# Holding one result in weight tiles, three heads in one 12 KB tile, and zeroing one shared scratch tensor once

## The chip, the cores and the metric

The kernel runs on one core of one Trainium2 chip. The metric is the device time of one execution in microseconds, the median of several runs. A profile of one further execution shows every instruction with its start and duration.

## The reference

Input is x of shape (4, 384, 32, 32): four images ("batches"), 384 channels, 1024 tokens each. Two layers follow one another, each with a residual around a mixing part and around a feed-forward part.

```python
# layer 0
x = x + L0_conv(ln_c(x))      # four-direction selective scan, 16 states, then layernorm and GELU
t = tokens(x)
t = t + L0_ffn(ln_t(t))       # 4 experts, top 2 per token: y = gelu(t w1 + b1) w2 + b2, weighted by the gate
# layer 1
x = x + L1_conv(ln_c(x))      # attention with 8 heads of 64; queries, keys and values share one projection
t = t + L1_ffn(ln_t(t))       # W = kron(c_fc_1, c_fc_2); gelu(t W^T) times kron(c_proj_1, c_proj_2)^T
```

The scan of layer 0 is `h = h * exp(dt * A) + dt * u * B`, `y = h . C`, over 1024 positions in each of four directions. All arithmetic is float32.

## The kernel before

The four batches go through two parts. The **scan** (`scan_layer`, `chunk`) takes a batch in 8 units (4 directions by 2 halves of the tokens); a unit has 3 channel chunks of 4 steps, so a batch has 96 steps. In a step POOL multiplies the scanned input with B (L440) and part of the states with C (L468), ACT makes the decay (L449), DVE runs the recurrence (L454) and the other products with C (L461), and PE adds the states up into `acc` (L475). Its inputs come back from DRAM in `dtr` (L424) and `bcs` (L350), issued by SP.

The **tail** (`tail_batch`) of a batch is everything else:

- `route`: `first` zeroes the scratch tensor `rows` (`clear`, L599, 19 DMAs of 192 KB) and turns the batch into token order; `second` chooses the experts, and POOL scatters each normalized token into its two rows of `rows` by indirect DMA (L685).
- `experts`: 11 slots, 8 of 256 rows and 3 of 128. A slot gathers its rows (`xs`, L925), loads an expert's weights as four `w1` tiles (L900) and four `w2` tiles (L908) of 576 KB each, computes `hs` (L954, L962, L967 or L959) and `y` (L975, L979), and writes `made` (L982).
- `combine` and `prologue`: POOL gathers the two results of each token (L1005), PE adds them with their gates (L1012), and the layernorm's result is transposed into `xc`.
- `attention`: four pairs of heads; each has a projection (weights L1069, matmuls L1076), scores (L1099), exponentials (L1105), the sum over values (L1145) and a division, into one `att` tile.
- `last_layers`: the output projection (L1198) with its residual gives `x2` (L1204); then the second feed-forward, in two halves of the tokens and two groups of hidden rows each (`hs`, L1259, L1265, L1268; L1276; L1284), whose result is added to `x2` (L1286) and stored (`out`, L1287). Its weights are `wa`, `wb` and `wc` (L1169 to L1173). For batches 0 and 1 the next batch's `route` steps stand inside it.

The tail of batch b runs beside the scan of batch b + 1. The tail of batch 3 comes last and uses a larger set of buffers (`WIDE`).

Tiles of the tail come from pools by tag, each with a number of buffers. A tile takes a buffer that is free, and its first writer waits until the last reader of what was there is done.

```python
NARROW = {"kw": 8, "k12": 2, "k4": 5, "got": 1, "bb": 2}
WIDE = {"kw": 10, "k12": 3, "k4": 4, "got": 2, "bb": 2}
...
att = room.tile([P, L], "kw", "att")
x2 = room.tile([P, DC, L], "k12", "x2")
hs = room.tile([P, FC, size], "k12", "hs")
```

"kw" tiles hold 4.5 KB a partition: the experts' weights, `wa`, `wb`, `wc`, projections, `got` and `att`. "k12" tiles hold 12 KB: `hs`, the combined tokens, `xc`, squares and `x2`.

The order of each engine's instructions is fixed at build time by a planner that simulates the program's progress. Parts marked with `high_priority` come earlier in it. On the chip each engine, and SP's queue of DMA issues, goes through its list strictly in order. The second branch of `build`, `second_layer_exact`, runs only if a softmax sum overflows; it doesn't run here, and the constant `EXACT` belongs to it.

Of the kernel before, what the change touches and what calls it, by code (L numbers as in the profile page):

```python
# [9 lines left out]
F32 = mybir.dt.float32  # L10
# [7 lines left out]
P = 128  # L18
# [62 lines left out]

NARROW = {"kw": 8, "k12": 2, "k4": 5, "got": 1, "bb": 2}
WIDE = {"kw": 10, "k12": 3, "k4": 4, "got": 2, "bb": 2}
EXACT = {"kw": 4, "k12": 2, "k4": 4, "got": 2}

FORWARD = 20000

# [28 lines left out]
class Body:  # L116
# [430 lines left out]
    def moe_consts(self, room):  # L547
        nc, a, wp = self.nc, self.a, self.const


        turn = wp.tile([P, DC, P + NE], F32, tag="turn", name="turn")
        wg = turn[:, :, P:]
        nc.sync.dma_start(out=wg, in_=a["wg"].rearrange("(c p) e -> p c e", p=P))
        for c in range(DC):
            nc.vector.tensor_copy(turn[:, c, :P], self.ident)
        ps = room.bank("p", "wg_ps")
        for c in range(DC):
            nc.tensor.matmul(ps[:, :NE], self.ones, wg[:, c, :], start=(c == 0), stop=(c == DC - 1))
        for c in range(DC):
            nc.vector.scalar_tensor_tensor(  # L560
                wg[:, c, :], ps[:, :NE], -1.0 / D, wg[:, c, :], op0=ALU.mult, op1=ALU.add
            )
        self.turn = turn
        bg = wp.tile([P, NE], F32, tag="bg", name="bg")
        nc.sync.dma_start(out=bg, in_=a["bg"].partition_broadcast(P))
        self.bg = bg

        def count(name, shape, pattern, base=0, channel=0):
            i = wp.tile([P, *shape], I32, tag=name, name=name + "_i")
            nc.gpsimd.iota(i, pattern=pattern, base=base, channel_multiplier=channel)  # L570
            f = i.bitcast(F32)
            nc.vector.tensor_copy(f, i)
            return f


        before = count("before", [P], [[1, P]], channel=-1)
        nc.vector.tensor_scalar(before, before, 0.0, None, op0=ALU.is_gt)
        self.before = before
        lower = count("lower", [NE, NE], [[1, NE], [-1, NE]])
        nc.vector.tensor_scalar(lower, lower, 0.0, None, op0=ALU.is_gt)  # L580
        self.lower = lower
        self.full = count("full", [L // P], [[P, L // P]])
        self.slot_at = count("slot_at", [NSLOT], [[1, NSLOT]])


        size = NROW
        self.zero = wp.tile([P, P], F32, tag="zero", name="zero")
        nc.gpsimd.memset(self.zero, 0.0)
        self.rows, self.made = [], []
        for b in range(B):  # L590
            self.rows.append(self.dram.tile([size, D], F32, tag=f"rows{b}", name=f"rows{b}"))
            self.made.append(self.dram.tile([size, D], F32, tag=f"made{b}", name=f"made{b}"))

    def clear(self, b):

        nc = self.nc
        self.zeroed = []
        for at in range(0, NROW, P):
            ins = nc.sync.dma_start(  # L599
                out=self.rows[b][at : at + P, :].rearrange("p (c d) -> p c d", c=DC),  # L600
                in_=self.zero.unsqueeze(1).to_broadcast([P, DC, P]),
            ).ins
            self.depend(ins, self.under_way[b])
            self.zeroed.append(ins)
# [8 lines left out]
    def route(self, b, x1, room):  # L613

        def forward():
            return nullcontext() if 0 < b < B - 1 else self.tc.high_priority(offset=FORWARD)

        parts = self.spread(b, x1, room)

        def first():  # L620
            self.clear(b)
            with forward():
                next(parts)

        def second():
            with forward():
                self.place, self.slots = next(parts)

        return first, second

    def spread(self, b, x1, room):
# [44 lines left out]
        for m in range(MB):  # L676
            if m % 2 == 0:
                xt = room.tile([P, 2, D], "k4", "xt")
                nc.sync.dma_start(out=xt, in_=self.tokens(b)[:, m : m + 2, :])
            nc.scalar.activation(  # L680
                xt[:, m % 2, :], xt[:, m % 2, :], AF.Identity,
                bias=less[:, m : m + 1], scale=rstd[:, m : m + 1],
            )
            for k in range(TOP):
                put = nc.gpsimd.indirect_dma_start(  # L685
                    out=self.rows[b][:, :],
                    out_offset=bass.IndirectOffsetOnAxis(ap=pos[:, k, m : m + 1], axis=0),
                    in_=xt[:, m % 2, :], in_offset=None,
                ).ins
                for other in placed:  # L690
                    self.tc.declare_no_dep(put, other, reason="rows of different tokens")
                for other in self.zeroed:
                    self.depend(put, other)
                placed.append(put)
        yield (pos, gate), (expert, placed)

    def places(self, sc, room):
# [184 lines left out]
    def experts(self, b, routed, room):  # L882

        nc, a = self.nc, self.a
        rows, made = self.rows[b], self.made[b]
        expert, placed = routed
        nw = 4
        wf = FC // nw
# [32 lines left out]
        def gather(s):  # L921
            at, size = extent(s)
            xs = room.tile([P, size // P, D], "k4", "xs")
            queue = nc.scalar if s == 0 else nc.sync
            got = queue.dma_start(  # L925
                out=xs, in_=rows[at : at + size, :].rearrange("(t p) d -> p t d", p=P)
            ).ins
            for put in placed:
                self.depend(got, put)
            xc = room.tile([P, DC, size], "k4", "xc")  # L930
            for lo in range(0, DC, HF // size):
                ps = room.bank("p", "xc_ps").rearrange("p (r l) -> p r l", l=size)
                n = min(HF // size, DC - lo)
                for c in range(lo, lo + n):
                    for t in range(size // P):
                        nc.tensor.transpose(  # L936
                            ps[:, c - lo, t * P : (t + 1) * P], xs[:, t, c * P : (c + 1) * P],
                            self.ident,
                        )
                nc.vector.tensor_copy(xc[:, lo : lo + n, :], ps[:, :n, :])  # L940
            return xc
# [116 lines left out]
    def attention(self, xc, sums, room):  # L1058
# [68 lines left out]

        steps = [(t, i, j) for t in range(HEADS // 2) for i in range(NH) for j in range(MB)]
        made = [project(0)]
        ahead = scores(0, made[0][0], 0, 0, None)  # L1130
        atts = []
        for n, (t, i, j) in enumerate(steps):
            ex, (early, last) = ahead
            if i == 0 and j == 0:
                atts.append(room.tile([P, L], "kw", "att"))
                if t + 1 < HEADS // 2:
                    made.append(project(t + 1))
            if n + 1 < len(steps):
# [19 lines left out]
    def last_layers(self, b, att, room, between=()):  # L1158
# [23 lines left out]
            self.cols[:, lo:hi].unsqueeze(1).to_broadcast([P, KR, KJ]),  # L1182
        )

        x2 = room.tile([P, DC, L], "k12", "x2")
        zt = room.tile([P, NH, HF], "k4", "z")
        zs = [zt[:, i, :] for i in range(NH)]
        for i in range(NH):
# [4 lines left out]
            for c in range(DC):  # L1193
                ps = room.bank("p", "o_ps")
                chunk = slice(c * P, (c + 1) * P)
                for t in range(nt):
                    w = wa[:, t, chunk] if t < nt - 1 else wb[:, 0, chunk]
                    nc.tensor.matmul(ps, w, att[t][:, halves(i)], start=(t == 0), stop=False)  # L1198
                for j in range(HF // P):
                    nc.tensor.matmul(  # L1200
                        ps[:, j * P : (j + 1) * P], part[j // 2][:, j % 2, chunk], self.ident,
                        start=False, stop=(j == HF // P - 1),
                    )
                nc.scalar.activation(  # L1204
                    x2[:, c, halves(i)], ps, AF.Identity, bias=self.col("bout", c)
                )
            mean = room.bank("p", "x2_mean")
            for c in range(DC):
                nc.tensor.matmul(
                    mean, self.ones, x2[:, c, halves(i)], start=(c == 0), stop=(c == DC - 1)  # L1210
                )
            sq = room.tile([P, DC, HF], "k12", "x2_sq")
            for c in range(DC):
                nc.vector.scalar_tensor_tensor(
                    sq[:, c, :], mean, -1.0 / D, x2[:, c, halves(i)], op0=ALU.mult, op1=ALU.add
                )
                nc.scalar.activation(sq[:, c, :], sq[:, c, :], AF.Square)
            zp = room.bank("p", "z_ps")
            for c in range(DC):
                nc.tensor.matmul(  # L1220
                    zp, wz[:, c * P : (c + 1) * P], x2[:, c, halves(i)],
                    start=(c == 0), stop=(c == DC - 1),
                )
            var = room.bank("p", "x2_var")
# [46 lines left out]
        for i in range(NH):  # L1271
# [10 lines left out]
            for c in range(DC):  # L1282
                ps = room.bank("p", "fo_ps")
                nc.tensor.matmul(ps, pj2[:, c * P : (c + 1) * P], y, start=True, stop=True)  # L1284
                o = room.tile([P, HF], "k4", "out")
                nc.vector.tensor_add(o, ps, x2[:, c, halves(i)])  # L1286
                nc.sync.dma_start(out=a["out"][b][c * P : (c + 1) * P, halves(i)], in_=o)  # L1287

    def second_layer_exact(self):
# [235 lines left out]
```

## Time and profile before

| | |
|---|---|
| median of 3 runs | 4242.87 us (4242.76 to 4247.99) |
| the profiled execution | 4230.72 us |
| its span, first to last instruction | 4228.9 us |
| mean granted TensorE clock | 0.873 of full speed |
| busy: PE, DVE, ACT, POOL | 3363.3, 2846.4, 2505.9, 3020.1 us |
| DMA | 693.70 MB; HBM read 569.00 MB, written 121.50 MB |
| `rows<-zero` | 76 issues of 192.0 KB on SP |

Busy time is the sum of instruction durations on an engine; the instructions that issue DMAs are not in it. The page also cuts the span into 40 equal slices and gives for each the busy share of an engine in tenths. In a group of instructions the row has the source line, engine, operation, output and input tiles, the count, the total and mean duration, and the engine's idle time just before them with what ended most of it.

### The profile page before, as it was taken

The numbers are of one execution on the slowest core, as the hardware profiler recorded it, in microseconds if no ns is written. First come the engines' busy times: TensorE is split into PE (matmuls) and PEld (weight loads), VectorE is DVE, ScalarE is ACT, GpSimd is POOL, SyncE is SP. The second block draws the span as 40 slices with busy tenths as digits, with TensorE's granted clock in tenths as the row PEclk, the third lists the DMA queues.
The fourth block names the chain that finished last, engine by engine and source line by source line (L and its number), as shares of the span: only waits on it lengthen the run. The fifth ranks groups of instructions, "written<-read, shape, count | busy, mean of one in ns | idle before, by whom it ended". The sixth has DMA issues, their size and how long they took to land.

```text
span 4228.9 us, 45721 instructions
## 1 busy us (share of the span) xinstructions
PE 3363.3 (80%) x13308; PEld 1581.4 (37%) x13308; DVE 2846.4 (67%) x4152; ACT 2505.9 (59%) x4494; POOL 3020.1 (71%) x1471
## 2 busy tenths in 40 slices
PE   6544545489897888789996888789996899999898
PEld 2111111155553223245553223245553235566323
DVE  5999997878887878788887777888886840010101
ACT  5555555556665776666665777676664763443353
POOL 5999997898988978789899878889897840000100
PEclk8666666589998999789997999789997899999999
DMA  5454464677886535667887434658887434255200
GB/s 138 125 135 123 117 174 109 187 218 218 242 249 176 153 106 147 198 178 230 251 247 220 130 100 133 200 166 242 227 250 225 117 107 143 86 174 209 64 16 31
DMA packets 410387, 693.70 MB, mean 164 GB/s; under 512 B 51088, under 2 KB 209680, under 8 KB 410128
## 3 DMA queue, kind: packets, MB, share of 16 engines
q1 hardware_dynamic: 399728, 662.71, 54.1%
q0 software_dynamic: 8192, 25.17, 1.8%
q10 hardware_dynamic: 2208, 2.82, 0.2%
q8 instruction: 107, 1.75, 0.2%
q14 instruction: 152, 1.25, 0.1%
HBM read 569.00 MB, written 121.50 MB: 163 GB/s over the span
## 4 chain that ended last, share of the span: by engine, by line
PE 37%; DVE 22%; ACT 11%; DMA 11%; POOL 9%; issue 7%; SPq 3%; DVEq 0%; POOLq 0%; ACTq 0%
PE y_ps L975 9%; PE h_ps L954 9%; DVE da L454 8%; DVE bx L454 7%; POOL bx L440 5%; DMA dtr<-dd 4%; ACT da L449 3%; PE s_ps L1099 3%; PE acc L475 3%; DVE bx L461 3%; PE o_acc L1145 3%; POOL bx L468 2%; DMA w<-in_w 2%; SPq L424 2%; DMA bcs<-both 1%
## 5 line engine op out<-in xcount | busy, mean ns | idle before, releaser
L440 POOL TENSOR_TENSOR bx<-dtr,bcs 128x1024 f32<-128x1024 f32 x768 | 1794.0, 2363 | 201.6 <-PE acc L475 92.4
L449 ACT ACTIVATE da<-dtr,nega 128x512 f32<-128x512 f32 x1536 | 1045.3, 690 | 898.3 <-DVE bx L461 540.9
L468 POOL TENSOR_TENSOR bx<-bx,bcs 128x1024 f32<-128x1024 f32 x384 | 905.1, 2362 | 133.3 <-DVE carry L465 60.5
L475 PE MATMUL acc<-bx,sel 128*32 128x512 f32 x3072 | 500.2, 697 | 294.0 <-POOL bx L468 256.8
L954 PE MATMUL h_ps<-xc,w 128*128 128x256 f32 (+1 forms) x3168 | 675.8, 370 | 71.0 <-DMA w<-in_w 40.0
L975 PE MATMUL y_ps<-w,hs 128*128 128x384 f32 x1824 | 634.4, 500 | 26.7 <-ACT hs L967 20.1
L954 PEld LDWEIGHTS h_ps<-xc,w 128*128 128x128 f32 x3168 | 561.0, 201 | 240.7 <-issue 120.2
L454 DVE TENSOR_TENSOR_SCAN bx<-da,carry,bx 128x512 f32<-128x512 f32 x384 | 473.5, 1270 | 112.9 <-ACT da L449 57.7
L454 DVE TENSOR_TENSOR_SCAN da<-da,carry,bx 128x512 f32<-128x512 f32 x384 | 477.3, 1275 | 60.9 <-ACT da L449 50.2
L454 DVE TENSOR_TENSOR_SCAN bx<-da,bx 128x512 f32<-128x512 f32 x384 | 453.5, 1211 | 90.4 <-ACT da L449 56.8
L461 DVE TENSOR_TENSOR bx<-da,bcs 128x512 f32<-128x512 f32 x768 | 511.0, 681 | 4.0
L454 DVE TENSOR_TENSOR_SCAN da<-da,bx 128x512 f32<-128x512 f32 x384 | 456.1, 1219 | 76.6 <-ACT da L449 64.8
L975 PEld LDWEIGHTS y_ps<-w,hs 128*128 128x128 f32 x1824 | 348.4, 195 | 306.2 <-issue 64.7
L1105 ACT ACTIVATE ex<-s_ps 128x512 f32<-128x512 f32 x512 | 300.8, 592 | 130.1 <-PE s_ps L1099 126.6
L1099 PE MATMUL s_ps<-w 64*128 64x512 f32 x1024 | 310.6, 664 | 61.6 <-ACT ex L1105 56.3
L962 ACT ACTIVATE hs<-h_ps,bb 128x256 f32<-128x256 f32 (+1 forms) x528 | 200.5, 441 | 212.4 <-PE h_ps L954 208.2
L996 POOL TENSOR_TENSOR diag<-ident,g_weight 128x1024 f32<-128x1024 f32 x8 | 15.0, 1896 | 424.3 <-PE xc_ps L936 410.6
L1145 PE MATMUL o_acc<-ex,vt 128*64 128x512 f32 x1024 | 284.7, 633 | 24.0 <-ACT ex L1105 16.8
L475 PEld LDWEIGHTS acc<-bx,sel 128*32 128x32 f32 x3072 | 75.8, 116 | 594.1 <-POOL bx L468 361.7
L979 DVE TENSOR_TENSOR y<-y_ps,bb 128x384 f32<-128x384 f32 x76 | 41.6, 547 | 230.9 <-PE y_ps L975 230.6
L1099 PEld LDWEIGHTS s_ps<-w 64*128 64x128 f32 x1024 | 83.8, 190 | 267.2 <-ACT ex L1105 219.0
L365 PE MATMUL dt_ps<-xd,wdt 108*128 108x512 f32 x192 | 123.1, 728 | 63.4 <-ACT mag L404 34.4
(222 smaller groups left out, 3613.0 us busy)
## 6 DMA issues: line engine op xcount, KB each, us to landing
w<-in_w SPq DMA_DIRECT2D x352, 576.0 KB
dtr<-dd SPq DMA_DIRECT2D x1536, 128.0 KB
bcs<-both SPq DMA_DIRECT2D x512, 128.0 KB
dd<-one_e SPq DMA_DIRECT2D x96, 256.0 KB
dd<-mag SPq DMA_DIRECT2D x96, 256.0 KB
rows<-zero SPq DMA_DIRECT2D x76, 192.0 KB
xt<-x SPq DMA_DIRECT2D x32, 384.0 KB
made<-y SPq DMA_DIRECT2D x32, 384.0 KB
```

What stands on the lines that cost most here:

```text
L440: pool = nc.gpsimd.tensor_mul(bx, dtr[q][1], bc[:, 0].unsqueeze(1).to_broadcast([P, 2, HF])).ins
L449: nc.scalar.activation(da, dtr[q][0][:, j, :], AF.Exp, scale=nega[:, col : col + 1])
L454: nc.vector.tensor_tensor_scan(run(h), run(da), run(bx[:, j, :]), 0.0 if first else hold, ALU.mult, ALU.add,)
L461: dve = nc.vector.tensor_mul(bx[:, j, :], h, cg).ins
L468: pool = nc.gpsimd.tensor_mul(bx, bx, cg.unsqueeze(1).to_broadcast([P, 2, HF])).ins
L475: nc.tensor.matmul(acc[lo : lo + DB, :], sel, out[q][:, j, :], start=(g == 0), stop=(g == NG - 1),)
L954: ins = nc.tensor.matmul(ps[:, r, :], w1[(f + r) // wf][:, c, (f + r) % wf * P : ((f + r) % wf + 1) * P], xc[:, c, :], start=(c == 0), sto ...
L962: done = nc.scalar.activation(hs[:, f + r, :], ps[:, r, :], AF.Gelu if last else AF.Identity, bias=bb[:, f + r : f + r + 1],).ins
L975: nc.tensor.matmul(out[:, :D], hs[:, f, t * P : (t + 1) * P], w2[f // wf][:, f % wf, :], start=(f == 0), stop=(f == FC - 1),)
L1099: ins = nc.tensor.matmul(ps, w[rows, j * P : (j + 1) * P], w[rows, halves(i)], start=True, stop=True).ins
L1105: done.append(nc.scalar.activation(ex[:, o, :], ps, AF.Exp, scale=HD**-0.5, accum_out=sums[:, t, 2 * j + o, i : i + 1],).ins)
L1145: ins = nc.tensor.matmul(out[cols, :], made[t][1][:, j, cols], ex[:, o, :], start=(j == 0), stop=(j == MB - 1),).ins
```

## The change

Three things are changed. There is one `rows` tensor for all batches, zeroed once for batch 0; a later batch scatters over what the one before left there, and its first scatter waits for the earlier batch's gathers (`taken`). `x2` lies in three "kw" tiles in place of one "k12" tile. The `att` results of the first three head pairs are slices of one "k12" tile, and only the last is a "kw" tile. `EXACT` gets more "kw" buffers, since the branch that doesn't run shares `last_layers`.

```diff
-EXACT = {"kw": 4, "k12": 2, "k4": 4, "got": 2}
+EXACT = {"kw": 7, "k12": 2, "k4": 4, "got": 2}
...
-        self.rows, self.made = [], []
+        self.rows = self.dram.tile([size, D], F32, tag="rows", name="rows")
+        self.made, self.zeroed, self.taken = [], [], []
         for b in range(B):
-            self.rows.append(self.dram.tile([size, D], F32, tag=f"rows{b}", name=f"rows{b}"))
             self.made.append(self.dram.tile([size, D], F32, tag=f"made{b}", name=f"made{b}"))
...
         def first():
-            self.clear(b)
+            if b == 0:
+                self.clear(b)
             with forward():
                 next(parts)
...
-                for other in self.zeroed:
+                for other in self.zeroed + self.taken:
                     self.depend(put, other)
                 placed.append(put)
+        self.zeroed, self.taken = [], []
...
             for put in placed:
                 self.depend(got, put)
+            self.taken.append(got)
...
         made = [project(0)]
+        most = room.tile([P, HEADS // 2 - 1, L], "k12", "att")
...
             if i == 0 and j == 0:
-                atts.append(room.tile([P, L], "kw", "att"))
+                atts.append(
+                    most[:, t, :] if t < HEADS // 2 - 1 else room.tile([P, L], "kw", "att")
+                )
...
-        x2 = room.tile([P, DC, L], "k12", "x2")
+        x2 = [room.tile([P, L], "kw", "x2") for _ in range(DC)]
```

Every later use of `x2[:, c, halves(i)]` becomes `x2[c][:, halves(i)]`.

More of the change, by code (lines that the diff above doesn't have):

```diff
@@ L596, in clear @@
         nc = self.nc
-        self.zeroed = []
         for at in range(0, NROW, P):
             ins = nc.sync.dma_start(
-                out=self.rows[b][at : at + P, :].rearrange("p (c d) -> p c d", c=DC),
+                out=self.rows[at : at + P, :].rearrange("p (c d) -> p c d", c=DC),
                 in_=self.zero.unsqueeze(1).to_broadcast([P, DC, P]),
@@ L685, in spread @@
                 put = nc.gpsimd.indirect_dma_start(
-                    out=self.rows[b][:, :],
+                    out=self.rows[:, :],
                     out_offset=bass.IndirectOffsetOnAxis(ap=pos[:, k, m : m + 1], axis=0),
@@ L884, in experts @@
         nc, a = self.nc, self.a
-        rows, made = self.rows[b], self.made[b]
+        rows, made = self.rows, self.made[b]
         expert, placed = routed
@@ L1204, in last_layers @@
                 nc.scalar.activation(
-                    x2[:, c, halves(i)], ps, AF.Identity, bias=self.col("bout", c)
+                    x2[c][:, halves(i)], ps, AF.Identity, bias=self.col("bout", c)
                 )
@@ L1209, in last_layers @@
                 nc.tensor.matmul(
-                    mean, self.ones, x2[:, c, halves(i)], start=(c == 0), stop=(c == DC - 1)
+                    mean, self.ones, x2[c][:, halves(i)], start=(c == 0), stop=(c == DC - 1)
                 )
@@ L1214, in last_layers @@
                 nc.vector.scalar_tensor_tensor(
-                    sq[:, c, :], mean, -1.0 / D, x2[:, c, halves(i)], op0=ALU.mult, op1=ALU.add
+                    sq[:, c, :], mean, -1.0 / D, x2[c][:, halves(i)], op0=ALU.mult, op1=ALU.add
                 )
@@ L1220, in last_layers @@
                 nc.tensor.matmul(
-                    zp, wz[:, c * P : (c + 1) * P], x2[:, c, halves(i)],
+                    zp, wz[:, c * P : (c + 1) * P], x2[c][:, halves(i)],
                     start=(c == 0), stop=(c == DC - 1),
@@ L1285, in last_layers @@
                 o = room.tile([P, HF], "k4", "out")
-                nc.vector.tensor_add(o, ps, x2[:, c, halves(i)])
+                nc.vector.tensor_add(o, ps, x2[c][:, halves(i)])
                 nc.sync.dma_start(out=a["out"][b][c * P : (c + 1) * P, halves(i)], in_=o)
```

## The prediction

> **What bounds the kernel now.** I read the page's slices first, then its groups, then timeline, waits and chain at the places that the diff touches.
>
> ```profile
> PE   6544545489897888789996888789996899999898
> POOL 5999997898988978789899878889897840000100
> PEclk8666666589998999789997999789997899999999
> ...
> L440 POOL TENSOR_TENSOR bx<-dtr,bcs 128x1024 f32<-128x1024 f32 x768 | 1794.0, 2363 | 201.6 <-PE acc L475 92.4
> ```
>
> A slice is 105.7 us. Up to slice 32 (about 3430 us) POOL is the fullest engine: its two multiplies are 1794.0 + 905.1 = 2699 us. From slice 31 on PE is at 90% or more almost without a break. So there are two stages with different limits: four scans paced by POOL with the previous batch's tail woven in, then 800 us of PE. Time saved before about 3270 us passes on to the end; time saved by ACT or POOL after it hardly does.
>
> The zeroing of `rows` (L599) stands in the first stage, on SP. Its three later bursts, from the timeline of SP:
>
> ```profile
> 1413.94 12.86 SPq L599 DMA_DIRECT2D rows<-zero  x19
> ...
> 2313.90 13.33 SPq L599 DMA_DIRECT2D rows<-zero  x19
> ...
> 3205.08 4.88 SPq L599 DMA_DIRECT2D rows<-zero  x2
> 3210.06 1.31 SPq L982 DMA_DIRECT2D made<-y  x1
> 3211.42 14.39 SPq L599 DMA_DIRECT2D rows<-zero  x17
> ```
>
> Nothing else leaves SP meanwhile, and it issues nearly every load. What stood behind the bursts, from the timelines of PE and POOL and the waits of ACT:
>
> ```profile
> 2333.05 7.09 PE L1076 MATMUL w_ps<-xc,wqkv 128*128 128x512 f32 x12 [8.98 <-DMA wqkv<-in_wqkv]
> ...
> 2338.89 1.27 POOL L395 TENSOR_TENSOR mag<-one_e,mag 128x512 f32<-128x512 f32 x1 [7.86 <-ACT one_e L382]
> ...
> ACT da L449 <- DMA dtr<-dd: 8.1, 1, 8.1
> ```
>
> The bracket is idle time before the instruction and what ended it. At burst 2 PE, with both scan and attention in its queue, waits 8.98 us for attention weights issued at 2329.4, right behind the burst. At burst 3 ACT waits 8.1 us (3222 to 3230) for scan rows issued after it. At burst 1 POOL worked on until 1427.3; its waits nearby (1.68 and 4.17 us) are put down to DVE and PE, not to a load.
>
> **The change part by part.** The sum is made against the profiled execution: 4228.9 us of span in 4230.7 us. The median of the runs shown is 4242.9, 12.2 above; I add that at the end.
>
> *Zeroing.* 57 of 76 issues and 57 x 192 KB = 11.2 MB of writes go (12.86 + 13.33 + 19.27 us of SP). Burst 1: between 0 (POOL not starved) and 4.2 us (if PE's delay came from loads behind it); I take 2. Burst 2: 9.0, PE's wait; POOL's 7.86 overlaps it and isn't added. Burst 3: 8.1, ACT's wait; the upper end is 19.3, all of the issue time, since the chain of waits runs through this burst to the scan's `dtr` loads and POOL's gathers of `made`. Together -19.1, between -8 (nothing at burst 1, half caught up later, since POOL has some 10% to spare) and -33. What is late next, once the burst is gone, is at burst 2 nothing on PE (its queue reaches `w_ps` at 2324), at burst 3 the five multiplies that POOL has queued ahead of its gathers.
>
> *One `rows` tensor.* A batch's first scatter (POOL) now waits for the previous batch's ten gathers instead of its own nineteen clears. The scatter of batch 3 begins near 3472, and the last gather of batch 2 was issued at 3174.6. Those waits are met by some 300 us; the cover is batch 2's last slots and most of its attention. Cost 0; if it were gone, all of POOL's scan would queue behind it.
>
> *Three heads' results in one 12 KB tile.* No instruction is added. It takes the buffer that the combined tokens leave, and `att` gives up three weight tiles, so `wc` (L1173) can be loaded earlier: 30, 6 and 13 places in SP's order for batches 0, 1 and 2, the removed zeroing left out of the count. DVE waited for it (L1180) 0.6 us in batch 0 and 4.7 us in batch 1. Between -5.3 (both go) and 0 (six places are few); I take -2.
>
> *`x2` in three weight tiles.* The same instructions, other addresses. Freed is a 12 KB buffer for `hs` through the FFN. In the built order of PE it buys nothing: the first slot's transposes still come behind the FFN's last matmul (place 2370 against 2366 before), and the FFN spans the same 86 matmul places. Gain 0; if the double buffer did let it in earlier, the most is PE's idle time there, 5.0 us (`xc_ps` waits at 1824.7) at each of two entries.
> What it moves: of a first slot's four `w2` loads (L908), three used to go out long before the FFN's end, now all four stand behind its last three or so `out` stores, for batches 1 and 2. Before:
>
> ```profile
> 1762.76 2.85 SPq L908 DMA_DIRECT2D w<-in_w  x3
> ...
> 1821.72 0.36 SPq L908 DMA_DIRECT2D w<-in_w  x1
> ...
> 1825.32 0.37 SPq L925 DMA_DIRECT2D xs<-rows  x1
> ...
> 1867.86 2.52 PE L975 MATMUL y_ps<-w,hs 128*128 128x384 f32 x7
> ```
>
> Each SP issue is 0.95 us here, so 2.9 us more stand ahead of the second slot's `xs` and 16 scan loads; the 3 x 576 KB at about 240 GB/s (the rate of the busy FFN stretch 1835 to 2260) are 7.2 us of transfer. `w2` is first used at 1867.9, some 30 us after it can have landed, so PE doesn't wait for it. The scan loads may: between 0 (DMA was 48% busy between 1820 and 1835, so there is room; and 104% busy between 1760 and 1775, where the three leave) and 7.2 us at each entry, 14.4 together; a gain of as much is possible at 1763. I take +1 for both.
> A rule of the Trainium skill speaks against this part. The row first: SP's own waits put 89.6 us on L908 waiting for PE's y_ps, 35 times. The page "DMA: Bandwidth & Descriptors", section on the anatomy of one DMA, says that the transfer engines never wait on semaphores; the issuing sequencer does, before dispatch. So a `w2` load whose tile `x2` still holds would stop all of SP. By the rule alone each entry could cost SP's whole wait, 11.4 us for `out` at the first entry; by the rows the `out` stores ahead of it already wait for the same DVE additions, so nothing is added. I follow the rows.
>
> *Tables.* ACT's order has two table loads more. At scan 3's two finishes an `Exp` now stands inside each group of three `Gelu` (L230): four more loads; at the end of batch 2's experts two fewer. The row, on the chain of waits:
>
> ```profile
> 3431.14 1.28 ACT L230 ACT_TABLE_LOAD   x1
> 3432.43 2.23 ACT L230 ACTIVATE y<-y,cols 128x512 f32<-128x512 f32 x3
> ```
>
> Two at 1.28 are +2.6. The Trainium skill ("ScalarE: Activation LUTs", what ACT_TABLE_LOAD costs) adds a drain and counts 2.66 for a switch: +5.3. Here the next activation starts 1.29 us after the load began, so the row decides; the rule would make the whole 2.7 us worse.
>
> *Order.* Removing DMAs makes the planner lay out everything from the first attention on anew. The work is the same, so only idle time can change. The size comes from the trace itself: the first slots of batches 0, 1 and 2 begin (xc_ps) at 862.5, 1824.7 and 2793.4, so two periods of equal work in different orders took 962.2 and 968.7. Their difference, 6.5 us, over three periods adds as 6.5 x 1.7 = 11 us either way (an estimate). I take 0.
>
> Sum: -19.1 - 2 + 1 + 2.6 + 0 = -17.5. 4230.7 - 17.5 = 4213.2; with the 12.2 us of the shown median, 4225.4, say 4226.
>
> **The rivals.**
> *Caught up.* Bursts delay only work that had slack. For it: at burst 1 POOL didn't starve, and POOL is at 9 tenths, not 10. Against: at bursts 2 and 3 three engines stood idle at once. Then -21.1 shrinks to about -4, while tables and `w2` keep their 3.6: 4242.9 - 4 + 3.6 = 4242.5.
> *The tail is queued behind more of the scan (slower).* The planner believes that the scan runs ahead without the bursts, and has put more of it in front of the tail on PE: at batch 2's last slot (L936) 1448 instead of 1436 `acc` matmuls come first, at its combine (L1012) 1464 instead of 1460. Four such matmuls are one step of the scan; three batches of 96 steps took from 667.0 to 3354.8 (first x1 stores), 9.3 us a step. So the last slot waits for up to 28 us of scan, the combine for 9.3. It costs something if the real scan at 3190 is less than those one to three steps ahead, which needs most of the 19 us above to come true; if it doesn't, PE idles until POOL has caught up, and the PE-bound rest starts late. Price: midway, 19 us, with the tables and no gain: 4243 + 19 + 3 = 4265. For it: tail and scan share every in-order queue. Against: at the combine only one step is left.
> *The sharing works after all:* first slots start inside the FFN: -10 more, 4216. PE's order speaks against it.
>
> **How the numbers follow.** The runs shown reach from 4242.8 to 4248.0, so about 0.2% (8.5 us) can be told from no change. Gain kept: 0.45 (of it 0.04 with under 8.5 us); sharing works too: 0.04; caught up: 0.16; tail behind the scan: 0.35, of it 0.01 within 0.2%. Faster 0.45, same 0.21, slower 0.34. The likeliest case alone: 4226, from 4209 (burst 3 at its upper end and a good order) to 4242. The range for 8 in 10 reaches from 4202 (that with most of the 10 us of sharing) to 4268 (the slower rival with part of the reordering).
>
> **What would show it.** Right: L599 has 19 issues, all near 534 us; PE's wait of 9 us for `wqkv` and ACT's 8.1 us for `dtr` at the former bursts are gone; the first slots of batches 1 and 2 start up to 5 us earlier, that of batch 3 about 15; the stage from there to the end is as long as before (within 3 us); HBM writes are about 11 MB less. Wrong: first x1 stores of batch 3 (3354.8) no earlier, or PE waits for POOL's `bx` in the last slots of batch 2 longer than before; `y_ps` of a first slot waiting for `w`; SP waiting at L908 for `out`, with POOL waiting for `dtr` after it.

## The result, and the profile after

The changed kernel is slower: 4263.02 us (4257.44 to 4269.47) against 4247.01 us (4242.76 to 4250.63) for the kernel before on the same chip, a ratio of 1.0046 with a 95% interval of 1.0032 to 1.006. The forecast was 4226. The profiled execution took 4262.08 us with a span of 4260.3 us, 31.4 us more than before's span.

From the page of the changed kernel, PE's row of busy times, the slices (now 106.5 us each) and POOL's larger multiply:

```profile
PE 3356.7 (79%) x13308; PEld 1577.9 (37%) x13308; DVE 2845.3 (67%) x4152; ACT 2510.5 (59%) x4496; POOL 3019.2 (71%) x1471
...
PE   6445544389897888689986888679897889999899
...
POOL 5999997898888978888988877889898930000100
PEclk8666666689998999689997999889998999999999
...
L440 POOL TENSOR_TENSOR bx<-dtr,bcs 128x1024 f32<-128x1024 f32 x768 | 1794.3, 2365 | 177.4 <-DMA dtr<-dd 78.2
```

The two stages are still there, and the engines that set the pace have no more to do: PE is busy for 3356.7 us (3363.3 before), POOL for 3019.2 (3020.1), and one multiply takes 2365 ns (2363). Only ACT has 4.6 us more. The 31 us are idle time of PE and POOL.

The waits that the prediction set out to remove are gone. One burst of zeroing is left (SP's timeline), the attention weights of batch 1 are there when PE wants them (PE's timeline; the bracket held 8.98 us of `wqkv` before), ACT's longest wait for `dtr` fell from 8.1 to 2.9 us (the waits of the whole span), and HBM writes are 11.2 MB fewer (the page; 121.50 before):

```profile
534.55 12.88 SPq L598 DMA_DIRECT2D rows<-zero  x19
```
```profile
2345.97 7.12 PE L1078 MATMUL w_ps<-xc,wqkv 128*128 128x512 f32 x12 [1.08 <-ACT xc L1057]
```
```profile
ACT da L449 <- DMA dtr<-dd: 37.8, 25, 2.9
```
```profile
HBM read 569.00 MB, written 110.30 MB: 159 GB/s over the span
```

Yet everything starts later, from batch 1's part on. The table gives the first or last instruction of a stage in both traces, in us from the start of the span.

| | before | after | later by |
|---|---|---|---|
| first slot of batch 1 (`xc_ps`) | 1824.7 | 1840.3 | 15.6 |
| combine of batch 1 (`w_ps<-got`) | 2272.9 | 2302.5 | 29.6 |
| first slot of batch 2 | 2793.4 | 2825.3 | 31.9 |
| last `xc_ps` of batch 2 | 3183.5 | 3245.0 | 61.5 |
| first x1 store of batch 3 | 3354.8 | 3380.8 | 26.0 |
| last `acc` of the scan | 3418.2 | 3436.7 | 18.5 |
| first slot of batch 3 | 3503.5 | 3531.1 | 27.6 |
| end | 4228.9 | 4260.3 | 31.4 |

About half of the 31.4 us is not the change's: before's profiled execution (4230.72) is 16 us under the median of 4247.01, the changed kernel's 1 us under its own. The medians differ by 16.0 us, and the table can't say in which stage those lie.

At the end of batch 1's experts POOL works on at the scan before it issues the gathers of `made`, and PE, which has the combine next in its list, waits for them. From the changed kernel's timelines of POOL and of PE:

```profile
2269.47 6.97 POOL L440 TENSOR_TENSOR bx<-dtr,bcs 128x1024 f32<-128x1024 f32 x3 [0.38 <-DMA dtr<-dd]
...
2297.79 1.01 POOL L1007 DMA_INDIRECT got<-made,g_pos  x1 [0.16 <-issue]
```
```profile
2243.01 0.87 PE L938 MATMUL xc_ps<-ident,xs 128*128 128x128 f32 x3 [5.18 <-DMA xs<-rows]
...
2302.47 1.62 PE L1014 MATMUL w_ps<-got,diag 128*128 128x384 f32 x2 [11.25 <-DMA got<-made,g_pos]
```

Before, the first of these gathers left at 2267.48, 30 us earlier, and PE took up its result without a wait:

```profile
2267.48 1.01 POOL L1005 DMA_INDIRECT got<-made,g_pos  x1
```
```profile
2272.87 2.61 PE L1012 MATMUL w_ps<-got,diag 128*128 128x384 f32 x4
```

The largest new wait of all, though, does not explain the loss. From SP's waits in the changed kernel:

```profile
SPq L1197 <- PE o_acc L1150: 117.1, 3, 112.4
```

All three lie after 3950 us, where little is left to load, and the fast redraw e4 below has the same row with the same 112.4 us.

### The profile page after: what moved, and what is told of

Its sections match the earlier page's. It is cut to its first block, busy times and chain, and to the rows that moved or that the text cites. A ratio compares the mean times of both kernels' runs of the same rounds, so it can differ in the third digit from the quotient of the medians.

```text
span 4260.3 us, 45636 instructions
## 1 busy us (share of the span) xinstructions
PE 3356.7 (79%) x13308; PEld 1577.9 (37%) x13308; DVE 2845.3 (67%) x4152; ACT 2510.5 (59%) x4496; POOL 3019.2 (71%) x1471
## 5 line engine op out<-in xcount | busy, mean ns | idle before, releaser
L440 POOL TENSOR_TENSOR bx<-dtr,bcs 128x1024 f32<-128x1024 f32 x768 | 1794.3, 2365 | 177.4 <-DMA dtr<-dd 78.2
L468 POOL TENSOR_TENSOR bx<-bx,bcs 128x1024 f32<-128x1024 f32 x384 | 906.2, 2365 | 151.9 <-DVE bx L454 72.2
L956 PE MATMUL h_ps<-xc,w 128*128 128x256 f32 (+1 forms) x3168 | 666.9, 366 | 65.6 <-DMA w<-in_w 27.9
L475 PE MATMUL acc<-bx,sel 128*32 128x512 f32 x3072 | 487.7, 696 | 290.8 <-POOL bx L468 258.5
```

What stands on the lines that cost most here:

```text
L440: pool = nc.gpsimd.tensor_mul(bx, dtr[q][1], bc[:, 0].unsqueeze(1).to_broadcast([P, 2, HF])).ins
L468: pool = nc.gpsimd.tensor_mul(bx, bx, cg.unsqueeze(1).to_broadcast([P, 2, HF])).ins
L475: nc.tensor.matmul(acc[lo : lo + DB, :], sel, out[q][:, j, :], start=(g == 0), stop=(g == NG - 1),)
L956: ins = nc.tensor.matmul(ps[:, r, :], w1[(f + r) // wf][:, c, (f + r) % wf * P : ((f + r) % wf + 1) * P], xc[:, c, :], start=(c == 0), sto ...
```

## The experiments

The theory after the result was that the order of instructions that the planner happened to lay out ("drew") lost more than the parts won. The rivals were that one of the parts, or the two together, cost time by themselves. Ratios are to the kernel before on the same chip, with 95% intervals; 0.001 is 4.2 us.

**Each part alone.** e1 has the one `rows` tensor and `taken`, with `x2` and `att` as before; e2 has the tiles and zeroes every batch as before.

```diff
 e1
-            self.clear(b)
+            if b == 0:
+                self.clear(b)
...
 e2
-        x2 = room.tile([P, DC, L], "k12", "x2")
+        x2 = [room.tile([P, L], "kw", "x2") for _ in range(DC)]
```

> Only the rows part of the change: one rows tensor, zeroed once; x2 and the heads' results stay as before. The orders of PE, ACT and POOL are those of before up to batch 1's attention, so burst 1 is taken away with nothing else changed. Theory A (the zeroing's removal gains, the loss comes from the other part): 10 to 20 us faster than before, with the gain at bursts 2 and 3. Theory B (the bursts delayed only work with slack, or the new order loses what they free): within 8 us of before. In both burst 1 is worth 0 to 4 us, seen at the end of batch 0's attention.

> Only the tile part: x2 in three weight tiles, three heads' results in a 12 KB tile; rows is zeroed for each batch as before. Theory A (this part loses by itself): 20 to 40 us slower than before, with the first slots of batches 1 and 2 late by 10 us and more each. Theory B (order and zeroing together lose): within 8 us of before.

e1: 4220.14 us, 0.9938 (0.9918 to 0.9958). e2: 4233.74 us, 0.9973 (0.9963 to 0.9983). Each part alone is faster than the kernel before, by 25.2 and 11.6 us of the medians (4245.36 for before); both gains are larger than any theory had expected. So neither part loses by itself, in the one order drawn for it. PE's order in e1 is that of the kernel before up to batch 1's attention and another after it; in e2 and in the changed kernel it leaves before's in batch 0's attention. Theory A wanted e1's gain at bursts 2 and 3. Its trace shows none at burst 2: batch 1's first slot starts at 1830.1, its combine at 2277.4 and batch 2's first slot at 2804.7, none earlier than in before's trace (which, though, lies 16 us under its median). The gain shows only behind burst 3: the scan's last `acc`, at 3402.7, is 15.5 earlier.

**The same work in another order.** One or more repeats of a DVE reduction in a division of the attention make the planner lay out what follows anew; such a kernel is called a redraw below. A repeat writes the same values again.

```diff
         def divide(t, att):
+            self.calls += 1
...
             nc.vector.tensor_reduce(inv, sums[:, t], AX.X, ALU.add)
+            for _ in range(4 if self.calls == 1 else 0):
+                nc.vector.tensor_reduce(inv, sums[:, t], AX.X, ALU.add)
```

The first pair has one repeat in batch 0's first division.

> The kernel before with one DVE reduction of 0.2 us repeated in batch 0's first division. It does the same work; the planner lays out everything from there on anew. Theory of order (a new layout alone moves the time, and the one before was a favourable one): 10 to 30 us slower than before. Theory of the parts (the time follows what is done, not its layout): within 8 us of before.

> The changed kernel with the same repeated reduction, so laid out anew in the same way. Theory of order: its time lies anywhere between 4225 and 4275 and differs from the changed kernel's 4263 by 10 us or more. Theory of the parts: within 8 us of 4263.

e3 (kernel before): 4240.69 us, 0.9984 (0.9974 to 0.9994). e4 (changed kernel): 4223.17 us, 0.9946 (0.9927 to 0.9964). e3 is 5 us faster, where the theory of order wanted 10 to 30 us slower; e4 differs from 4263 as that theory said, and lies just under its 4225. A reduction that adds work made the changed kernel some 40 us faster. In e4 the first gather of batch 1's results leaves POOL 33.5 us earlier than in the changed kernel (timeline of POOL in e4):

```profile
2264.27 1.01 POOL L1008 DMA_INDIRECT got<-made,g_pos  x1 [0.15 <-issue]
```

Is it the order, or the added instruction? In e5 the same single reduction stands one division later, where the order stays that of the changed kernel: in the two traces all 13308 matmuls of PE and all 2982 DMA issues of SP stand in the same order, and so do the instructions of ACT and POOL. e6 keeps the order up to batch 1's attention and redraws the rest. e7 and e8 are a second pair, with four repeats in the first division.

> The changed kernel with the same repeated 0.2 us reduction, but in batch 0's second division, where every engine's order stays as in the changed kernel. Theory of the order (the reduction only made the planner draw a better layout): the time stays at the changed kernel's 4263, within 4, and the losses stay where they were: combine of batch 1 starts 25 to 30 us later than before's, xc_ps of batch 2 about 30 later. Rival (the reduction itself, or where it shifts the code, makes the program quicker): 4223, as in the other redrawn kernel.

> The changed kernel with the reduction repeated four times in batch 1's first division: the order is the changed kernel's up to scan step 274 (batch 1's attention, after the 25 to 30 us are lost) and drawn anew from there. If the loss is made in batch 1's route and experts and only carried on: combine of batch 1 still starts 25 to 30 us later than before's, and the end is between 4240 and 4265. If it is mostly made later (scan 3 and batch 2's tail): the end comes back to 4215 to 4230.

> A second redraw of the changed kernel (four repeats in batch 0's first division; the order is new from scan step 168 on). Theory of the order: the changed kernel's 4263 is one unlucky draw of layouts that centre near 4223 (4245 less some 20 for the zeroing and the tiles), so this one comes out between 4210 and 4245. Rival (the two parts together cost by themselves, and the first redraw was the lucky one): 4255 to 4270.

> The same four repeats in the kernel before. Theory of the order: layouts of the kernel before centre near 4245 with a spread of some 15, so 4230 to 4260, and the distance to the changed kernel with the same repeats is about 20. If the spread is larger than the parts' effect, the two redrawn kernels differ by under 8 us or the other way round.

On this chip the kernel before took 4273.24 us, so times have to be read by their ratios; the expectations in us were made for 4245.

- e5: 4280.97 us, 1.0020 (1.0009 to 1.0031). Slower than before, as the changed kernel is, though by 8 us and not the 16 expected; nowhere near e4's 0.9946. Batch 1's combine starts at 2298.5, 25.6 later than before's. The instruction is not what helped. But the same order had 1.0046 in the result: the two intervals do not meet, and 0.0026 (11 us) therefore separates two measurements of one order, taken apart from each other. Ratios of kernels that did not run side by side are no surer than that.
- e6: 4285.47 us, 1.0028 (1.0015 to 1.0041). Batch 1's combine starts at 2306.5. A new order from batch 1's attention on, one draw of it, did not bring the time back.
- e7 (changed): 4255.07 us, 0.9962 (0.9952 to 0.9973). e8 (before): 4281.92 us, 1.0026 (1.0014 to 1.0038). A pair 27 us apart, in favour of the change.

e5 and e7 differ by the place and the number of repeats of a 0.2 us reduction, and by order. Their stages up to the scan's last `acc` and from there on (windows of each trace: stretch, length, busy time of PE with its matmuls, PEld, DVE, ACT, POOL, then clock and DMA), e5 first:

```profile
2540.00:3446.00 906.00, 743.22 (x3079) 363.35 (x3075) 715.37 (x1028) 591.05 (x1030) 773.94 (x376) 0.91 0.63 181
3446.00:4290.00 844.00, 771.34 (x3081) 388.48 (x3077) 86.78 (x215) 356.09 (x761) 38.52 (x37) 0.96 0.31 104
```
```profile
2540.00:3445.00 905.00, 756.08 (x3169) 369.17 (x3167) 720.11 (x1039) 598.40 (x1048) 784.07 (x380) 0.91 0.63 183
3445.00:4290.00 845.00, 736.54 (x2950) 380.58 (x2949) 84.96 (x211) 340.96 (x719) 38.52 (x37) 0.97 0.31 103
```

(The second stretch reaches past the end of the span, where nothing is.) Both scans end at the same time. But e7 has put 90 matmuls more into the 900 us before that, beside the scan, and has 131 fewer left for the stage that PE alone bounds: 736.54 us of PE instead of 771.34. That is about the difference of the two ends, 4245.5 against 4277.8, in one row. (e7's profiled execution is its fastest; the medians lie 26 us apart.)

Two more pairs, with two repeats in the first division and with four in the third:

> A third redraw of the changed kernel (two repeats in batch 0's first division). Theory (the parts are worth about 20 us, and the order drawn adds or takes up to 20): a ratio to the kernel before of 0.990 to 1.000, and 8 to 35 us under the kernel before with the same repeats. Rival (the parts are worth nothing once the order is free, and the two pairs so far were chance): the pair differs by less than 8 us or the other way round.

> The kernel before with two repeats in batch 0's first division. Theory: a ratio between 0.996 and 1.004, above its changed partner by 8 to 35 us. Rival: within 8 us of the partner, or under it.

> A fourth redraw of the changed kernel (four repeats in batch 0's third division, so the order up to scan step 184 is the changed kernel's). Theory: a ratio of 0.990 to 1.000 and 8 to 35 us under its partner. Rival: within 8 us of the partner, or over it.

> The kernel before with four repeats in batch 0's third division. Theory: a ratio between 0.996 and 1.004, above its changed partner by 8 to 35 us. Rival: within 8 us of the partner, or under it.

e9: 4231.13 us, 0.9967 (0.9958 to 0.9977); its partner e10: 4252.33 us, 1.0021 (1.0007 to 1.0034); 21 us apart. e11: 4251.11 us, 1.0016 (0.9999 to 1.0033), outside what was expected; its partner e12: 4259.1 us, 1.0036 (1.0024 to 1.0048); 8 us apart, the least that the theory allowed and within the noise of the two.

| order | kernel before | changed | difference |
|---|---|---|---|
| as built | 1 | 1.0046 | +0.0046 |
| one repeat, division 1 (e3, e4) | 0.9984 | 0.9946 | -0.0038 |
| four repeats, division 1 (e8, e7) | 1.0026 | 0.9962 | -0.0064 |
| two repeats, division 1 (e10, e9) | 1.0021 | 0.9967 | -0.0054 |
| four repeats, division 3 (e12, e11) | 1.0036 | 1.0016 | -0.0020 |

Each redrawn pair ran side by side. In four out of four the change is faster, by 0.0044 on average, 18.7 us, three times clear of the noise. But the orders as built were a good one for the kernel before (0.0017 under the mean of its redraws, 1.0017) and the worst one of five for the changed kernel (0.0073 over the mean of its redraws, 0.9973). -0.0044 + 0.0073 + 0.0017 = +0.0046 must hold by the way the means are taken; it divides the result and tests nothing. The 0.0073 is not sharp: with e5's 1.0020 for the same order it is 0.0047, and with e6, a late redraw without a partner, among the redraws it is 0.0062.

**Which feature of the order?** The two fastest redraws of the changed kernel (e4, e7) have 1440 and 1444 of the scan's `acc` matmuls ahead of batch 2's combine in PE's list, the changed kernel 1464, and most of the orders that took longer 1460 to 1468. (These are the program's matmuls, four to a step; in the trace each stands as two.) That is the prediction's slower rival, a tail queued behind more of the scan; e1, fast with 1468, spoke against it. So only this was moved, by a priority for one batch's experts. In e14 the offset is 8000, in e15 it is `FORWARD` with b == 1, and e16 is e13's edit in the kernel before.

```diff
 e13
-        self.experts(b, self.slots, room)
+        with self.tc.high_priority(offset=1800) if b == 2 else nullcontext():
+            self.experts(b, self.slots, room)
```

> The changed kernel with a priority of 1800 for batch 2's experts: PE's order is unchanged up to them and has 1436 acc matmuls of the scan ahead of batch 2's combine, where the changed kernel has 1464. Theory T (the tail stands behind too much of the scan): 15 to 30 us under the changed kernel (a ratio to the kernel before of 0.997 to 1.000), with the PE matmuls left at the scan's end down from 3077 towards 2950. Theory C (lost earlier, in batch 1, and carried on): the changed kernel's ratio of 1.002 to 1.005.

> The same with priority 8000: 1384 acc matmuls ahead of batch 2's combine, some 20 scan steps fewer than in the changed kernel. Theory T: 20 to 40 us under the changed kernel if PE's remainder counts alone; if the scan is then held up by the tail (POOL waiting for PE's acc), the scan's end is 10 to 30 us later and the gain is no larger than in e13. Theory C: a ratio of 1.002 to 1.005.

> The changed kernel with batch 1's experts pulled ahead instead: 964 acc matmuls ahead of batch 1's combine for 1048, and 1408 ahead of batch 2's. Theory T: batch 1's combine starts well before 2270, batch 2's tail is ahead too, and the end is 20 to 40 us under the changed kernel (ratio 0.993 to 1.000). Theory C expects as much here, as the loss in batch 1 is gone; so C holds if this gains and e13 and e14 don't.

> The kernel before with the priority of 1800 for batch 2's experts: 1432 acc matmuls ahead of its combine for 1460. Theory T: 10 to 25 us under the kernel before (0.994 to 0.998), though nothing of the change is in it. Theory C, and the theory that only the changed kernel suffers from its order: 0.998 to 1.002.

- e13: 4291.25 us, 1.0105 (1.0069 to 1.0141).
- e14: 4262.18 us, 1.0039 (1.0026 to 1.0051).
- e15: 4274.78 us, 1.0068 (1.0044 to 1.0091), although batch 1's combine starts at 2232.4, 40 us earlier than before's.
- e16: 4260.77 us, 1.0035 (1.0022 to 1.0048).

Theory T fell: none is clearly faster than the kernel whose tail it moves forward, and e13 and e16 are slower than theirs. Theory C, which expected e15 to gain, fell with it. What happens instead is a trade. e14's slices of POOL, and its two stages in the windows, then the changed kernel's two stages:

```profile
POOL 5999997898888978888988877876669992000100
```
```profile
2540.00:3538.00 998.00, 849.07 (x3586) 399.26 (x3579) 728.55 (x1047) 648.55 (x1206) 774.88 (x377) 0.93 0.58 168
3538.00:4290.00 752.00, 657.33 (x2579) 357.60 (x2577) 77.39 (x198) 293.77 (x586) 38.40 (x37) 0.95 0.33 112
```
```profile
2540.00:3437.00 897.00, 740.43 (x3084) 362.45 (x3081) 715.98 (x1030) 591.12 (x1032) 774.08 (x377) 0.91 0.64 183
3437.00:4290.00 853.00, 770.59 (x3077) 389.80 (x3075) 86.80 (x215) 355.28 (x761) 38.44 (x37) 0.97 0.31 102
```

Against the changed kernel 498 matmuls have left the last stage (3077 there), which is 94 us shorter: 4267.2 - 3537.6 = 729.6, for 823.6. But the scan ends 101 us later, at 3537.6 for 3436.7: POOL, which paces it, drops to 6 tenths for three slices while the tail has PE. From POOL's waits between 2850 us and the scan's end, e14 first and then the changed kernel:

```profile
POOL bx L440 <- PE acc L475: 79.1, 12, 16.6
```
```profile
POOL bx L440 <- PE acc L475: 3.3, 4, 1.4
```

In e13 the trade is worse: 55 us later for 30 us shorter; in e15 it is 83 later for 70 shorter. How many scan matmuls stand ahead of the tail went with the good orders, but moving that alone did not make one. Which of their details is the cause stays open. One candidate was not tested: the granted clock goes with the time. In the executions of the kernel before, on each of the five chips of e1 to e18, 0.001 less of the mean clock goes with 2.0 to 2.6 us more, and the mean over the executions is 0.8784 in e4, 0.8737 for the kernel before beside it and 0.8715 in the changed kernel. Whether an order is slow because of its clock, or has the lower clock because PE waits, no run here tells.

**The zeroing at an unchanged order.** e1's 25 us could be the zeroing or its order. With four repeats in the first division PE's order with and without the zeroing is the same up to batch 2's combine (e17 against e8); with two repeats, until just behind batch 1's (e18 against e10). The edits are e1's and the redraw's together.

> The rows tensor zeroed once, and nothing else of the change, with four repeats in batch 0's first division. PE's order is that of the kernel before with the same repeats (ratio 1.0026) up to the 1464th acc matmul. Theory (the zeroing costs 19 us of waits, whatever the order): a ratio of 0.9965 to 0.9995. Rival (the gain of the first rows-only kernel was its order): 1.001 to 1.004.

> The same with two repeats; its partner, the kernel before with two repeats, had a ratio of 1.0021, and the order is the same up to the 1056th acc matmul. Theory: 0.996 to 1.000. Rival: 1.000 to 1.004.

e17: 4248.76 us, 1.0007 (0.9994 to 1.0021), 0.0019 under e8. e18: 4249.55 us, 1.0013 (1.0001 to 1.0025), 0.0008 under e10. By that the zeroing is worth 8 and 3 us, and with intervals of 0.0012 to 0.0014 on each side neither is told from nothing; e17 and e18 also ran on another chip than e8 and e10. The theory that it saves 19 us in any order is not borne out. In e8, the wait behind the second burst was short already (PE's waits):

```profile
PE w_ps L1077 <- DMA wqkv<-in_wqkv: 3.0, 1, 3.0
```

So most of e1's 25 us was probably its order too.

## Why the prediction was wrong, step by step

- **Zeroing, -19.1: mechanism right, size wrong.** The bursts, the waits behind them and 11.2 MB of writes went as said. At an order that is the same past the second burst, that bought 3 to 8 us, if anything. The three waits of one trace (2, 9.0 and 8.1) were added up as if nothing were caught up later and as if any order had them; in e8 the 9.0 were 3.0. The rival "caught up" was closer on this term.
- **One `rows` tensor, 0.** As said, nothing in the traces speaks of a cost: in the changed kernel the scatters (L685) wait for no gather, and e1, which has the one tensor, is the fastest of all. (A batch has eleven gathers, not ten: 44 in all, 40 from SP and 4 from ACT.)
- **Three heads' results, -2; `x2`, +1; tables, +2.6.** DVE's 4.7 us for `wc` went. Its waits for `wb`, which the prediction left out, fell too, from 25.3 to 12.0 us; the longest of them, in batch 2's tail after the scan, from 23.6 to 12.0. The trace has two table loads more, 143 for 141, and 183.5 us of them for 180.9: right. In sum these terms were +1.6. Alone, in e2, the tiles gained 11.6 us, and e7 and e9 stand 0.0045 and 0.0046 (19 us) under e17 and e18, which lack only the tiles; each time with another order and on another chip, so that how much is the tiles' own was not separated.
- **The first slots** of batches 1 and 2 came 15.6 and 31.9 us later, not up to 5 earlier, and batch 3's 27.6 later, not 15 earlier. The first x1 store of batch 3 at 3380.8 for 3354.8 was the first of the signs named as "wrong". That sign does not tell slow from fast, though: in e4, faster than before, the store is late as well, at 3371.4.
- **The stage from batch 3's first slot to the end** took 729.2 us for 725.4, just outside the 3 us given. (PE reaches 90% from slice 33 on; slices 31 and 32, which the prediction counts with them, are at 6 and 8 tenths. That changes no term.)
- **Order, taken as 0 with 11 us either way: the step that failed.** The redraws put the changed kernel's order 31 us over the mean of its others (20 us by e5), and before's 7 under its own. The 11 us came from two periods of one program that differed by 6.5 us. Those belong to the same draw and say little about another. Where the new order loses is in part shown (batch 1's gathers leave POOL 30 us later than before, 33.5 later than in e4); what in the order does it stays open. Measured over five orders each, the kernel before spans 22 us (0.9984 to 1.0036) and the changed one 42 (0.9946 to 1.0046), either of them more than the 17.5 that the other terms come to. With an order term of that size the sum could not tell faster from slower, and the forecast should not have leaned on the zeroing.
- **The slower rival, 4265**, named nearly the measured time by luck, since the experiments refused its mechanism. Only through it did the range of 4202 to 4268 hold the measured time. In the trace PE does not wait longer for POOL's `bx` in batch 2's last slots; and with the tail moved ahead of the scan (e13 to e16) the kernels got slower or stayed where they were.

## What to carry to other kernels

Where a planner lays out the program, an edit is two changes: the edit, and a new draw of the order. Before a difference of half a per cent is credited to the edit, redraw both versions a few times with a harmless instruction, run each pair side by side, and compare the means; here this turned +0.46% into -0.44%. And where two stages share in-order queues, moving work ahead is a trade: read the end of the paced stage and the work left after it side by side.

## What the runs showed that was not expected

- A repeated reduction makes the changed kernel 40 us faster through order alone, and the same reduction one division later, where the order stays, does not.
- The faster versions are e1 (0.9938) and e4 (0.9946). Both are draws: other orders of the same work gave 1.0007 and 1.0013 for e1, and 0.9962 to 1.0046 for e4.
- One program's executions spread more than the effect: the kernel before ranged from 4233.41 to 4263.5 us on one chip, and its medians beside these kernels were 4243.94 to 4247.01, but 4273.24 on the chip of e5 to e8. The profiled execution on which the prediction was built (4230.72) lies under all 44 of the executions on that one chip.
